# Neighbour lists for a graph network: the second half of each list is traced one list later

## The chip, the cores and the metric

The kernel runs on one core of one Trainium2 chip. The metric is the device time of one execution in microseconds; less is better. Times of the kernel before: 2126.52 us, median of 3 runs (2125.99 to 2130.2).

## The reference

Two layers of graph attention over 4096 nodes, each with a residual and a layer norm. The adjacency matrix is given dense (4096 x 4096 integers), but it is sparse and its density falls with the row and the column number. Cut to what matters here:

```python
e = leaky_relu(f2[:, :, None] + f1[:, None, :], 0.2)     # per head, 4096 x 4096
e = where(adj[None] > 0, e, NEG_INF)
att = softmax(e, axis=-1)
out = einsum('knm,kmp->knp', att, h)                     # h = x @ W, per head
x = layernorm(x + out)                                   # layer 0; layer 1 has two
                                                         # such attentions and two dense layers
```

`adj` is random with probability proportional to 1 / sqrt((i + 1)(j + 1)), so the first 128 rows have up to some hundred neighbours each, the last 128 rows up to two dozen.

## The kernel before

The kernel does not compute the dense 4096 x 4096 scores. A first stage, `find_edges`, turns every block of 128 rows of `adj` into a list of its edges; the three attention layers after it gather the neighbours' rows by these lists. A last stage does the two dense layers. (A dense path exists for inputs that don't fit the lists; a flag chooses it at run time, and it is not taken here.)

`find_edges` handles 35 lists, counted v = 0 to 34 here: the first block of 128 rows is cut into four column ranges (lists 0 to 3), and every block after it is one list (lists 4 to 34, row blocks 1 to 31). k is the most neighbours of a row in a list (104 or 112 in lists 0 to 3, then 56 down to 24), and n the number of chunks of 128 edges that the list takes (12 or 13, then 21 down to 5).

The way of one list, with the lines of the code and the engine that does each step:

- First half. The 2 MB of a row block come in as integers, and ScalarE makes signs of them (`sg`, L848). TensorE makes keys (L877 adds the signs, L878 the column's place) in PSUM, 1024 columns at a time, in two buffers, with four matmuls of 512 columns each. VectorE takes the eight largest keys of every segment of columns (`cand`, L884; in lists 0 to 3 three times, with replacements, L887), and then the k largest of these in order (`lst`, L899 and L901). ScalarE makes of them the column numbers (`qs`, L906) and, by signs with a running sum (L909), the number of neighbours; GpSimd makes the counts of it in six or seven small steps (L911 to L926).
- Second half. TensorE adds up the counts of the rows ahead of each row (`prs`, L931, the prefix sum). ScalarE makes the start and end of each row's edges and, of both, `sides` (L932 to L943); GpSimd adds the two sides to `s1` (L944). ScalarE and GpSimd split `qs` into two bf16 parts (L952 to L955). TensorE multiplies both by `s1` (`pl`, L960 to L969), which gives each edge its row's data, in pieces of at most 512 columns; `pl` has one PSUM buffer. ScalarE copies the node number (`nl`, L971) and for the long lists `kk` (L984). VectorE picks each edge's neighbour (`sel`, L977 to L981, or L986 for lists 0 to 3), and GpSimd writes `hole` and `idx` (L972, L992 to L994), which the gathers use.

Beside the last list of each row block, `beside(t)` loads that block of x, transposes it and multiplies it by the first layer's weights (L683 to L717).

The order of the instructions within this stage isn't written by hand. The tile framework's scheduler sets it when the kernel is built: it walks through the program by estimated durations and gives each engine, whenever that engine is free, the ready instruction that was traced first. What comes out is one fixed queue for each engine. The stages after `find_edges` are traced with `manual_schedule`, so their order is that of the code. There the first gathers are those of row block 31, which is the last list to be made.

Of the kernel before, what the change touches and what calls it, by code (L numbers as in the profile page):

```python
# [10 lines left out]
F32 = mybir.dt.float32  # L11
BF16 = mybir.dt.bfloat16
# [3 lines left out]
AF = mybir.ActivationFunctionType  # L16
OP = mybir.AluOpType
AX = mybir.AxisListType
# [3 lines left out]
P = 128  # L22
N = 4096
# [20 lines left out]
FAR = -1e30  # L44
# [514 lines left out]
def sparse_path(  # L559
# [23 lines left out]
    nc = tc.nc  # L583
# [6 lines left out]
    most = max(p.blocks for p in pts)  # L590
    longest = max(p.n for p in pts)
    kmax = max(p.k for p in pts)
# [8 lines left out]
    ident_b = const.tile([P, P], BF16, name="s_identb")  # L601
# [10 lines left out]
    half = const.tile([P, 2], F32, name="half")  # L612
# [10 lines left out]
    s1 = const.tile([P, blocks_ * P], BF16, name="s1")  # L623
# [227 lines left out]
    def find_edges(big, sb, ps, pk, constants, sg, beside):  # L851
# [8 lines left out]
        starts = big.tile([P, nv], F32, name="starts")  # L860
        ends = big.tile([P, nv], F32, name="ends")
        degsum = big.tile([P, 1], F32, name="degsum")

        for v, p in enumerate(pts):
            t, k, c0, nch = p.t, p.k, p.first, p.n
            if t > 0:
# [28 lines left out]
            last = cand.rearrange("p (s e) -> p s e", e=r8)[:, skip:, r8 - 1]  # L895
# [9 lines left out]
            qs = sb.tile([P, kmax + 1], F32, name="qs")[:, : k + 1]  # L905
# [4 lines left out]
            deg = degs[:, v : v + 1]  # L910
# [16 lines left out]
            else:  # L927
                nc.gpsimd.tensor_copy(counts[:, v : v + 1], deg)
            deg = counts[:, v : v + 1]
            prs = ps.tile([P, 1], F32, name="prs", tag="small")  # L930
            nc.tensor.matmul(prs, before, deg, start=True, stop=True)  # L931
            nc.scalar.activation(qs[:, k:], prs, AF.Identity, bias=ends_at[:, v : v + 1], scale=-1.0)  # L932

            lim = sb.tile([P, 1], F32, name="lim")
            nc.gpsimd.tensor_sub(lim, deg, mids[:, v : v + 1])
            first = starts[:, v : v + 1]
            nc.scalar.activation(first, prs, AF.Identity, bias=mids[:, v : v + 1], scale=-1.0)
            nc.scalar.activation(ends[:, v : v + 1], prs, AF.Identity, bias=lim)
            wide = p.blocks * P
            here = s1[:, p.at * P : p.at * P + wide]  # L940
            sides = sb.tile([P, 2, most * P], BF16, name="sides")[:, :, :wide]
            nc.scalar.activation(sides[:, 0], iota_e[:, :wide], AF.Sign, bias=first)
            nc.scalar.activation(sides[:, 1], iota_e[:, :wide], AF.Sign, bias=ends[:, v : v + 1], scale=-1.0)  # L943
            nc.gpsimd.tensor_add(here, sides[:, 0], sides[:, 1])  # L944


            rhs = sb.tile([P, 2 * (kmax + 2)], BF16, name="rhs")[:, : 2 * (k + 2)].rearrange("p (h w) -> p h w", h=2)
            rest = sb.tile([P, 2 * (kmax + 1)], BF16, name="rest")[:, : 2 * (k + 1)].rearrange("p (h w) -> p h w", h=2)
            q2 = sb.tile([P, 2 * (kmax + 1)], F32, name="q2")[:, : 2 * (k + 1)].rearrange("p (h w) -> p h w", h=2)
            shape = [P, 2, k + 1]  # L950
            for h in range(2):
                nc.scalar.activation(rhs[:, h, : k + 1], qs, AF.Copy, scale=half[:, h : h + 1])  # L952
            nc.gpsimd.tensor_mul(q2, qs[:, None, :].to_broadcast(shape), half[:, :, None].to_broadcast(shape))
            nc.gpsimd.tensor_sub(rest, q2, rhs[:, :, : k + 1])
            nc.gpsimd.tensor_copy(rhs[:, :, k + 1], row1)  # L955
            per = 512 // (k + 2)
            for lo in range(0, nch, per):
                m = min(per, nch - lo)
                pl = ps.tile([P, m, k + 2], F32, name="pl")
                nc.tensor.matmul(  # L960
                    pl, ident_b, own_b[:, None, kmax - k :].to_broadcast([P, m, k + 2]), start=True, stop=False
                )
                last = None
                for block, groups, chunks in blocks_in(p, lo, m):
                    for of, w in ((rhs, k + 2), (rest, k + 1)):
                        if last:
                            nc.tensor.matmul(*last, start=False, stop=False)
                        last = pl[:, chunks, :w], s1[:, ts(p.at + block, P)], of[:, groups, :w]
                nc.tensor.matmul(*last, start=False, stop=True)  # L969
                cs = slice(c0 + lo, c0 + lo + m)  # L970
                nc.scalar.copy(nl[:, cs], pl[:, :, k + 1])  # L971
                nc.gpsimd.tensor_scalar(hole[:, cs, 0], nl[:, cs], -0.5, FAR, op0=OP.is_lt, op1=OP.mult)  # L972
                src = sb.tile([P, longest], F32, name="src")[:, :m]
                sel = sb.tile([P, 512], F32, name="sel")[:, : m * k].rearrange("p (m k) -> p m k", k=k)
                if k < 100:
                    shape = [P, m, k]
                    nc.vector.tensor_tensor(  # L977
                        sel, iota_k[:, lo : lo + m, :k], pl[:, :, k : k + 1].to_broadcast(shape), op=OP.is_equal
                    )
                    nc.vector.tensor_tensor(sel, sel, pl[:, :, :k], op=OP.mult)  # L980
                    nc.vector.tensor_reduce(src, sel, AX.X, OP.add)  # L981
                else:
                    kk = sb.tile([P, longest], F32, name="kk")[:, :m]
                    nc.scalar.copy(kk, pl[:, :, k])  # L984
                    for c in range(m):
                        nc.vector.scalar_tensor_tensor(  # L986
                            sel[:, c], iota_k[:, lo + c, :k], kk[:, c : c + 1], pl[:, c, :k],
                            op0=OP.is_equal, op1=OP.mult, accum_out=src[:, c : c + 1],
                        )

                past = sb.tile([P, longest], F32, name="past")[:, :m]
                nc.gpsimd.tensor_scalar(past, nl[:, cs], -0.5, 2.0 * N, op0=OP.is_lt, op1=OP.mult)  # L992
# [377 lines left out]
    with ExitStack() as pools:  # L1370
        big = pools.enter_context(tc.tile_pool(name="eb", bufs=1))
        sb = pools.enter_context(tc.tile_pool(name="es", bufs=2))
# [3 lines left out]
        ps = pools.enter_context(tc.tile_pool(name="ep", bufs=1, space=PSUM))  # L1376
# [21 lines left out]
    sb = ctx.enter_context(tc.tile_pool(name="ls", bufs=2, reuse_waits="tile"))  # L1398
# [30 lines left out]
    with tc.tile_pool(name="tb", bufs=1, side="right", reuse_waits="tile") as big, \  # L1429
# [95 lines left out]
        for last, block in zip(blocks, blocks[1:]):  # L1525
            chunks = sum(u.n for u in units if u.t in block)
# [91 lines left out]
```

## Time and profile before

| | |
|---|---|
| median of the runs | 2126.52 us |
| the profiled execution, its own time | 2338.45 us |
| its span | 2336.3 us |
| granted TensorE clock, mean | 0.879 |
| busy: PE / DVE / ACT / POOL | 76% / 57% / 28% / 49% |
| `find_edges`, by the trace | from the start to about 505 us |
| busy in its first 505 us: PE / DVE / ACT / POOL | 354.70 / 372.16 / 297.44 / 216.18 us |

PE is TensorE (PEld its weight loads), DVE VectorE, ACT ScalarE, POOL GpSimd, SP the engine that issues most DMAs. In an answer of the trace a name such as `cand<-key` says what is written and what is read. A wait is given as "engine tile line <- the engine, tile and line that ended it". In a timeline each row has the start, the duration, the engine, the line, the operation, the tiles with their shapes, and in square brackets how long the engine was idle before it and what ended that. The profiled execution is about a tenth longer than the median of the runs.

### The profile page before, as it was taken

To read this page: it belongs to the slowest core of one execution; us is meant where nothing else is said; L and a number is where in the kernel's file an instruction comes from. 1 tells how busy PE (TensorE), PEld (TensorE's weight loads), DVE (VectorE), ACT (ScalarE), POOL (GpSimd) and SP (SyncE) were. 2 spreads that over 40 slices of the span, in tenths; PEclk is the share of its full clock that TensorE was granted. 3 is DMA by queue.
4 is the path that set the end of the run, shared out by engine and by line. 5 is a ranking of instruction groups with operands and counts; after the bars stand their busy time and mean duration, and the time that the engine had idled before them with its cause. 6 is when DMAs were issued, how large, how long until landed. Compare 5 with 4: busy or idle time off the path is not lost.

```text
span 2336.3 us, 29301 instructions
## 1 busy us (share of the span) xinstructions
PE 1771.7 (76%) x8987; PEld 1040.1 (45%) x8987; DVE 1331.3 (57%) x3933; ACT 660.7 (28%) x2316; POOL 1151.6 (49%) x1658
## 2 busy tenths in 40 slices
PE   4777776645677787764667687666999898998997
PEld 3655442213444564432444465434545443444444
DVE  5887777745676797744555676653343424334322
ACT  3446776650222222111222232211111011111221
POOL 5424444456555666536556666536355634445300
PEclk9889997866878899876788899887999998999999
DMA  6434565536666667526555556436254624335301
GB/s 214 132 129 158 219 241 220 213 83 179 181 175 182 197 208 224 166 76 163 154 140 145 159 158 186 133 110 191 85 156 126 172 82 148 101 109 150 90 19 51
DMA packets 132589, 351.94 MB, mean 151 GB/s; under 512 B 41922, under 2 KB 42954, under 8 KB 128454
## 3 DMA queue, kind: packets, MB, share of 16 engines
q0 software_dynamic: 74160, 206.25, 32.5%
q1 hardware_dynamic: 58262, 143.72, 17.3%
q8 instruction: 74, 1.21, 0.2%
q14 instruction: 93, 0.76, 0.1%
HBM read 347.31 MB, written 42.24 MB: 167 GB/s over the span
## 4 chain that ended last, share of the span: by engine, by line
PE 46%; DVE 16%; issue 13%; ACT 7%; another core or an unknown queue 7%; POOL 6%; DMA 4%; SPq 0%; DVEq 0%; POOLq 0%; ACTq 0%
PE acc L1220 15%; PE ph L697 11%; PE p L1495 10%; PE p L1507 5%; DVE g L1208 3%; POOL g L1084 2%; DMA xr<-sx_d 2%; DVE cand L884 2%; DMA g<-table_t,idx 2%; PE pt L683 1%; POOL s L944 1%; DVE cand L901 1%; DVE lst L899 1%; ACT sides L943 1%
## 5 line engine op out<-in xcount | busy, mean ns | idle before, releaser
L1084 POOL DMA_INDIRECT g<-table_t,idx x927 | 937.2, 1011 | 769.4 <-PE acc L1220 336.4
L1220 PE MATMUL acc<-g,sm 128*64 128x260 f32 (+2 forms) x4068 | 587.9, 414 | 175.3 <-DVE g L1208 91.7
L697 PE MATMUL ph<-sw_t,xt 128*128 128x264 f32 (+1 forms) x1536 | 436.4, 437 | 146.5 <-ACT xt L686 80.6
L1220 PEld LDWEIGHTS acc<-g,sm 128*64 128x64 f32 x4068 | 332.9, 146 | 395.1 <-issue 123.9
L697 PEld LDWEIGHTS ph<-sw_t,xt 128*128 128x128 f32 x1536 | 323.0, 217 | 229.2 <-ACT xt L686 97.9
L1208 DVE TENSOR_TENSOR g<-g,wp 128x2048 f32<-128x2048 f32 (+4 forms) x134 | 349.3, 2607 | 37.9 <-ACT wp L1163 18.7
L884 DVE MAX8 cand<-key 128x8 f32<-128x353 f32 (+55 forms) x467 | 196.3, 446 | 79.5 <-PE key L878 78.9
L1495 PE MATMUL p<-sht,sl1w 128*128 128x512 f32 (+1 forms) x576 | 229.0, 553 | 5.5 <-issue 4.9
L1507 PE MATMUL p<-sl2w,shid 128*128 128x512 f32 x512 | 227.2, 598 | 0.0
L686 ACT ACTIVATE xt<-pt 128x128 f32<-128x128 f32 x384 | 101.5, 279 | 292.9 <-PE pt L683 122.1
L710 ACT COPY hrow<-ph 128x260 f32<-128x260 f32 (+2 forms) x194 | 71.9, 374 | 320.2 <-PE ph L697 186.9
L1495 PEld LDWEIGHTS p<-sht,sl1w 128*128 128x128 f32 x576 | 107.7, 191 | 116.9 <-issue 112.0
L1507 PEld LDWEIGHTS p<-sl2w,shid 128*128 128x128 f32 x512 | 95.4, 190 | 120.4 <-issue 119.6
L1257 DVE SCALAR_TENSOR_TENSOR o<-ex,o 128x512 f32<-128x512 f32 x64 | 44.5, 695 | 179.2 <-ACT ex L1256 150.0
L877 PE MATMUL key<-sg,s_identb 128*128 128x512 bf16 (+1 forms) x258 | 111.9, 435 | 14.5 <-DVE cand L884 9.0
L848 ACT ACTIVATE sg<-raw 128x4096 bf16<-128x4096 int32 (+1 forms) x39 | 117.0, 2999 | 9.4 <-PE key L877 5.0
L1498 ACT ACTIVATE shid<-p,sl1b 128x512 f32<-128x512 f32 (+1 forms) x72 | 46.0, 640 | 244.5 <-PE p L1495 221.0
L878 PE MATMUL key<-frac,places 128*128 128x512 bf16 (+1 forms) x258 | 112.0, 435 | 2.6 <-POOL places L784 2.6
L1195 DVE TENSOR_SCALAR sm<-iota_n,nl,w 128x64 f32<-128x64 f32 x339 | 83.5, 328 | 31.9 <-ACT w L1166 31.9
L1155 DVE TENSOR_TENSOR z<-s,g 128x16 f32<-128x16 f32 (+9 forms) x294 | 44.7, 174 | 82.9 <-DMA g<-table_t,idx 81.2
L686 ACT ACTIVATION_READ_ACCUMULATOR xt<-pt 128x1 f32 x384 | 79.9, 208 | 0.0
L1228 DVE RECIPROCAL rd<-acc 128x8 f32<-128x8 f32 x64 | 13.1, 205 | 114.4 <-PE acc L1220 73.3
(184 smaller groups left out, 1812.8 us busy)
## 6 DMA issues: line engine op xcount, KB each, us to landing
raw<-in_adj_dram SPq DMA_DIRECT2D x31, 2048.0 KB
table_t<-hrow SPq DMA_DIRECT2D x64, 260.0 KB
xr<-in_x_dram SPq DMA_DIRECT2D x64, 256.0 KB
g<-table_t,idx POOLq DMA_INDIRECT x927
table_t<-hrow SPq DMA_DIRECT2D x32, 257.0 KB
sx_d<-o SPq DMA_DIRECT2D x32, 256.0 KB
xr<-sx_d SPq DMA_DIRECT2D x32, 256.0 KB
out_dram<-xr SPq DMA_DIRECT2D x32, 256.0 KB
```

The lines of the kernel that those rows point to most:

```text
L686: nc.scalar.activation(xt[:, c, :], pt[:, c, :], AF.Copy, accum_out=st.xparts[:, c, t : t + 1])
L697: nc.tensor.matmul(ph[:n], columns(c), st.w[:, c, j], start=(c == 0), stop=(c == FC - 1))
L848: nc.scalar.activation(sg[:, ts(i, w)], raw[:, ts(i, w)], AF.Sign)
L877: nc.tensor.matmul(out_, ident_b, sg[:, j:e], start=True, stop=False)
L878: nc.tensor.matmul(out_, places[:, w], frac[:, j - w * KW : e - w * KW], start=False, stop=True)
L884: nc.vector.max(out=cand[:, at : at + 8], in_=part)
L1084: nc.gpsimd.indirect_dma_start(out=u.g[:, k, : self.st.row], out_offset=None, in_=self.st.table[:, :], in_offset=bass.IndirectOffsetOnAxis ...
L1195: nc.vector.tensor_scalar(sm[:, at + i], of_g, node[k], u.w[:, k], op0=OP.is_equal, op1=OP.mult)
L1208: nc.vector.tensor_mul(body, body, wp[:, :, :, None].to_broadcast(body.shape))
L1220: nc.tensor.matmul(out_[g * HN : (g + 1) * HN], sm[:, slot], rows(k), start=start, stop=stop)
L1495: nc.tensor.matmul(p1, l1w[:, c, ts(k, P)], hts[b][:, c, :n], start=(c == 0), stop=(c == FC - 1))
L1507: nc.tensor.matmul(p2, hids[b][:, k, ts(j, P)], l2w[:, k, :], start=(k == 0), stop=(k == HC - 1))
```

## The change

The second half of each list is put into a function `place`, with all that it uses of its list bound as defaults. The function is kept in a list and called one list later: after the first half of list v + 1, and before `beside` of that list's block. The last one is called after the loop. No instruction is added, removed or altered, and no buffer; only the order in which they are traced. Cut to its core (the body of `place` is L930 to L994 as they were, moved right):

```diff
         degsum = big.tile([P, 1], F32, name="degsum")
 
+        places_of = []
         for v, p in enumerate(pts):
...
             deg = counts[:, v : v + 1]
-            prs = ps.tile([P, 1], F32, name="prs", tag="small")
-            nc.tensor.matmul(prs, before, deg, start=True, stop=True)
...
-                nc.gpsimd.tensor_add(past, past, src)
-                nc.gpsimd.tensor_copy(idx[:, cs], past)
+            def place(v=v, p=p, k=k, c0=c0, nch=nch, qs=qs, deg=deg):
+                prs = ps.tile([P, 1], F32, name="prs", tag="small")
+                nc.tensor.matmul(prs, before, deg, start=True, stop=True)
...
+                    nc.gpsimd.tensor_add(past, past, src)
+                    nc.gpsimd.tensor_copy(idx[:, cs], past)
+
+
+            places_of.append(place)
+            if len(places_of) > 1:
+                places_of.pop(0)()
             if p.last:
                 beside(t)
+        places_of.pop(0)()
```

More of the change, by code (lines that the diff above doesn't have):

```diff
@@ L929, in find_edges @@
             deg = counts[:, v : v + 1]
-            prs = ps.tile([P, 1], F32, name="prs", tag="small")
[L931 to L944, printed above, removed]
@@ L947, in find_edges @@
[L947 to L978, printed above, removed]
-                    )
[L980 to L988, printed above, removed]
-                        )
-                past = sb.tile([P, longest], F32, name="past")[:, :m]
-                nc.gpsimd.tensor_scalar(past, nl[:, cs], -0.5, 2.0 * N, op0=OP.is_lt, op1=OP.mult)
-                nc.gpsimd.tensor_add(past, past, src)
-                nc.gpsimd.tensor_copy(idx[:, cs], past)
@@ new lines, in place @@
+            def place(v=v, p=p, k=k, c0=c0, nch=nch, qs=qs, deg=deg):
+                prs = ps.tile([P, 1], F32, name="prs", tag="small")
+                nc.tensor.matmul(prs, before, deg, start=True, stop=True)
+                nc.scalar.activation(qs[:, k:], prs, AF.Identity, bias=ends_at[:, v : v + 1], scale=-1.0)
+                lim = sb.tile([P, 1], F32, name="lim")
+                nc.gpsimd.tensor_sub(lim, deg, mids[:, v : v + 1])
+                first = starts[:, v : v + 1]
+                nc.scalar.activation(first, prs, AF.Identity, bias=mids[:, v : v + 1], scale=-1.0)
+                nc.scalar.activation(ends[:, v : v + 1], prs, AF.Identity, bias=lim)
+                wide = p.blocks * P
+                here = s1[:, p.at * P : p.at * P + wide]
+                sides = sb.tile([P, 2, most * P], BF16, name="sides")[:, :, :wide]
+                nc.scalar.activation(sides[:, 0], iota_e[:, :wide], AF.Sign, bias=first)
+                nc.scalar.activation(sides[:, 1], iota_e[:, :wide], AF.Sign, bias=ends[:, v : v + 1], scale=-1.0)
+                nc.gpsimd.tensor_add(here, sides[:, 0], sides[:, 1])
+                rhs = sb.tile([P, 2 * (kmax + 2)], BF16, name="rhs")[:, : 2 * (k + 2)].rearrange("p (h w) -> p h w", h=2)
+                rest = sb.tile([P, 2 * (kmax + 1)], BF16, name="rest")[:, : 2 * (k + 1)].rearrange("p (h w) -> p h w", h=2)
+                q2 = sb.tile([P, 2 * (kmax + 1)], F32, name="q2")[:, : 2 * (k + 1)].rearrange("p (h w) -> p h w", h=2)
+                shape = [P, 2, k + 1]
+                for h in range(2):
+                    nc.scalar.activation(rhs[:, h, : k + 1], qs, AF.Copy, scale=half[:, h : h + 1])
+                nc.gpsimd.tensor_mul(q2, qs[:, None, :].to_broadcast(shape), half[:, :, None].to_broadcast(shape))
+                nc.gpsimd.tensor_sub(rest, q2, rhs[:, :, : k + 1])
+                nc.gpsimd.tensor_copy(rhs[:, :, k + 1], row1)
+                per = 512 // (k + 2)
+                for lo in range(0, nch, per):
+                    m = min(per, nch - lo)
+                    pl = ps.tile([P, m, k + 2], F32, name="pl")
+                    nc.tensor.matmul(
+                        pl, ident_b, own_b[:, None, kmax - k :].to_broadcast([P, m, k + 2]), start=True, stop=False
+                    )
+                    last = None
+                    for block, groups, chunks in blocks_in(p, lo, m):
+                        for of, w in ((rhs, k + 2), (rest, k + 1)):
+                            if last:
+                                nc.tensor.matmul(*last, start=False, stop=False)
+                            last = pl[:, chunks, :w], s1[:, ts(p.at + block, P)], of[:, groups, :w]
+                    nc.tensor.matmul(*last, start=False, stop=True)
+                    cs = slice(c0 + lo, c0 + lo + m)
+                    nc.scalar.copy(nl[:, cs], pl[:, :, k + 1])
+                    nc.gpsimd.tensor_scalar(hole[:, cs, 0], nl[:, cs], -0.5, FAR, op0=OP.is_lt, op1=OP.mult)
+                    src = sb.tile([P, longest], F32, name="src")[:, :m]
+                    sel = sb.tile([P, 512], F32, name="sel")[:, : m * k].rearrange("p (m k) -> p m k", k=k)
+                    if k < 100:
+                        shape = [P, m, k]
+                        nc.vector.tensor_tensor(
+                            sel, iota_k[:, lo : lo + m, :k], pl[:, :, k : k + 1].to_broadcast(shape), op=OP.is_equal
+                        )
+                        nc.vector.tensor_tensor(sel, sel, pl[:, :, :k], op=OP.mult)
+                        nc.vector.tensor_reduce(src, sel, AX.X, OP.add)
+                    else:
+                        kk = sb.tile([P, longest], F32, name="kk")[:, :m]
+                        nc.scalar.copy(kk, pl[:, :, k])
+                        for c in range(m):
+                            nc.vector.scalar_tensor_tensor(
+                                sel[:, c], iota_k[:, lo + c, :k], kk[:, c : c + 1], pl[:, c, :k],
+                                op0=OP.is_equal, op1=OP.mult, accum_out=src[:, c : c + 1],
+                            )
+                    past = sb.tile([P, longest], F32, name="past")[:, :m]
+                    nc.gpsimd.tensor_scalar(past, nl[:, cs], -0.5, 2.0 * N, op0=OP.is_lt, op1=OP.mult)
+                    nc.gpsimd.tensor_add(past, past, src)
+                    nc.gpsimd.tensor_copy(idx[:, cs], past)
```

## The prediction

> **What bounds the kernel now.** The change touches one stage only, the making of the neighbour lists, so I first looked for the stage's place in the span. The table of busy time by stretch (columns: stretch, its length, then busy time and count on PE, PEld, DVE, ACT and POOL, granted clock, DMA share, GB/s) gives it:
>
> ```profile
> 35.00:170.00 135.00, 101.69 (x478) 75.69 (x479) 114.61 (x532) 62.27 (x279) 45.15 (x96) 0.87 0.44 143
> 170.00:240.00 70.00, 56.09 (x344) 35.60 (x342) 51.73 (x196) 44.02 (x132) 32.64 (x108) 0.91 0.45 162
> 240.00:505.00 265.00, 185.43 (x896) 86.09 (x895) 189.42 (x612) 180.63 (x416) 112.84 (x423) 0.85 0.52 192
> ```
>
> The stage ends near 505 of 2336.3 us. The gathers of the next layer start with row block 31, whose list is finished last, so a microsecond saved before the last list is saved from the total. DVE is the fullest engine: 114.61 of 135.00 us (85%) in the four lists of row block 0, 189.42 of 265.00 (71%) from about the ninth list on. No engine and no DMA queue is full there, so I went to what the idle time waits for. The answer on waits, DVE alone and then PE alone, from 35 to 505 us (columns: total us, times, longest):
>
> ```profile
> DVE cand L884 <- PE key L878: 73.2, 59, 3.3
> DVE sel L986 <- ACT kk L984: 17.3, 10, 3.5
> DVE sel L977 <- ACT nl L971: 6.0, 6, 2.1
> ```
>
> ```profile
> PE pl L967 <- POOL s L944: 35.7, 32, 4.8
> PE prs L931 <- POOL counts L926: 33.8, 29, 2.1
> PE pl L960 <- DVE sel L980: 7.0, 7, 1.9
> ```
>
> DVE waits 73.2 us for keys that PE makes, while PE waits 35.7 + 33.8 us for steps of the second half (prs, pl). The keys are late because they stand behind a waiting prs or pl in PE's queue. The timeline shows it for row block 30, whose prs cuts one key pair of row block 31 in two:
>
> ```profile
> 484.59 0.63 PE L877 MATMUL key<-sg,s_identb 128*128 128x512 bf16 x1
> ...
> 485.70 0.59 PE L931 MATMUL prs<-counts,before 128*128 128x1 f32 x2 [0.48 <-POOL counts L926]
> ...
> 486.15 0.59 PE L878 MATMUL key<-frac,places 128*128 128x512 bf16 x1
> ...
> 486.78 1.30 DVE L884 MAX8 cand<-key 128x8 f32<-128x949 f32 x2 [1.85 <-PE key L878]
> ```
>
> The key matmuls around it follow one another at 0.43 us; the second of this pair starts 1.56 us after the first, and DVE loses 1.85 us. In row block 0 the same happens on DVE itself, where a sel step waits with maxima of the next list behind it:
>
> ```profile
> 48.50 0.23 DVE L887 MATCH_REPLACE8 left<-cand,left 128x85 f32<-128x85 f32 x1
> 50.97 0.32 DVE L986 SCALAR_TENSOR_TENSOR sel<-iota_k,kk,pl 128x104 f32<-128x104 f32 x1 [2.24 <-ACT kk L984]
> ...
> 51.95 0.25 DVE L884 MAX8 cand<-left 128x8 f32<-128x85 f32 x1
> ```
>
> **What the Trainium skill says.** "PSUM — Partial Sum Buffer", section "Engine vs sequencer instructions": the queues of ScalarE, VectorE and GpSimdE are strict FIFO, and matmuls start and complete in program order. The trace agrees: L878 at 486.15 follows the prs at 485.70 although its input was there. So what the scheduler writes down is what the chip waits in. "Perfetto Trace Analysis", section "Optimization Strategy": gaps that repeat can mean too few buffers for the next tile. pl has one buffer, and PE waits 7.0 us for it. "TensorE: Matmul & The Clock Gate", section "What's actually happening": the clock gate lets through half of the clock after an idle window. The trace has both speeds, key matmuls that start 0.43 us apart (484.17, 484.59) and 0.21 apart (477.77, 477.99), and a granted clock of 0.85 from 240 us on. No page prices a reordering.
>
> **The change, part by part.** It removes and adds no instruction. place(v), from prs to idx, is traced after the first half of list v+1 and before the projection beside it. Trace order is what the scheduler ranks by when two instructions are ready together, so place(v) now ranks below keys, maxima, sorted list and counts of list v+1 (and below the projection of its own block), and still above keys of list v+2. An engine without ready work of higher rank takes place(v) as before. place issues no DMA: no load or store on SP's queue and no gather on POOL's is passed. What is passed, engine by engine:
>
> *DVE, row block 0 (lists 0 to 3).* The ten waits of L986 are 17.3 us. Four are the first piece of a list (2.24, 1.44, 1.94 and 3.48, sum 9.1): the scheduler put them as soon as it held them ready, the chip was later. With lower rank they come only into gaps between a maximum and its replacement, so some max work goes ahead. The later pieces wait for one another through the single pl buffer, whatever their rank. I take half of 9.1: **-4.5 us**; bounds 0 (the gaps come at once) and -17.3 (every wait covered).
>
> *PE, lists 4 to 33.* I counted in the PE timeline how many of the 16 key matmuls of list v+1 precede prs of list v. A group that shares one key buffer is four matmuls, and in 18 of 30 lists the count is 8 or 12: the next group waits for a buffer and the rank decides nothing. In 12 lists it is 9, 10, 11, 13 or 14: there prs has cut into a ready group. After the change the one to three remaining matmuls (0.21 to 0.43 us each) go first and fill the wait for counts, 1.17 us on average (33.8 / 29), so prs isn't later, and DVE gets its keys up to 1.2 us earlier (73.2 / 59 is the mean wait): at most 12 x 1.2 = 14.4. But there is a second chain: pl(v) stands in front of keys(v+2), whose first maximum DVE takes before the sorted list of v+1, which leads to counts, prs and pl of v+1. Place(v) keeps its rank over keys(v+2), so this chain stays. I take half: **-7 us**; bounds 0 and -14.4.
>
> *DVE, lists 4 to 34.* sel(v) now ranks below the sorted list of v+1 (L899, L901). At its start two or three of the three L899 have already gone in most lists with k = 24, so it moves little there. The single pl buffer comes free later, and L960 of the next list waits at PE with keys behind it: today 7.0 us. If it moves by one L899/L901 pair, 0.5 us, in all 31 lists, it costs 15.5; the nearer value is a fifth: **+3 us**; bounds -1 and +15.5 (a wait for nl, 6.0 us in all, may also shrink).
>
> *ACT and POOL.* Seven short ACT steps and nine POOL steps of place rank below qs, signs and six small POOL steps of list v+1 (about 0.8 and 1.3 us). POOL is busy 112.84 of 265 us and the two groups lie several us apart, so I cost it at 0, hidden by POOL's idle time; if they met in every list, 31 x 1.3 = 40 us of delay would lie on place, which has nearly a list's time of slack. The 3.6 us sign step of list v+2 is in front of or behind place(v) exactly as before.
>
> *The end.* The sorted list of block 31 no longer shares DVE with sel of block 30 (three steps of 0.28, 0.26 and 0.27 us, today inside it): -0.5; bounds -1 and +2, if place(30) spills behind it. The last place itself has nothing to hide behind either way.
>
> Sum: -4.5 - 7 + 3 - 0.5 = **-9 us**. The durations come from the profiled execution, 2338.45 us by its own time for a span of 2336.3, and 10% above the median of 2126.52; I subtract the same microseconds from the median, since the page doesn't show which stage is longer under the profiler (scaled by 0.91 it would be -8): 2126.5 - 9 = about **2118 us**.
>
> **The rivals.**
> 1. *The order hardly moves* (21%). For it: 18 of 30 counts are 8 or 12, sel already comes after most of the sorted list, and engines with idle time take ready work whatever its rank. Against it: 12 cut groups and 17.3 us of waits for kk. Time 2126, within 4 us.
> 2. *The pl buffer becomes the wait* (33%), the case on the slower side. The place is L960 and L967 at the head of PE's queue. With sel(v) behind the sorted list of v+1, and in lists 4 to 6 (two or three pl pieces each, 0.4 to 0.65 us per sel step) behind up to a list's maxima, the bank comes free later than PE reaches it; keys of v+2 stand behind it, and DVE starves. One more wait of 0.5 us in 31 lists is 15.5 us; less the 2 us gained at row block 0 it is about 2140. It decides from the point where L980 of list v ends later than the last key group of v+1 on PE.
> 3. *The circle is cut* (9%). If the lists shift so that the first key group of v+2 goes ahead of pl(v), the chain above is broken for good and the list runs at DVE's busy time: half of 73.2 + 17.3 is 45 us, 2081. Against it: place(v) keeps its rank over keys(v+2).
>
> **How the numbers follow.** My own case has 37%. About 0.2%, 4.3 us, is what a measurement of this kernel can tell from no change. Faster by more: 31 of my 37, all 9 of rival 3, 3 of rival 1: 43%. Within: 6 + 14 + 2 of rival 2: 22%. Slower: 31 of rival 2 and 4 of rival 1: 35%. Range: my case alone reaches from 2103 (all gains near their ends) to 2124; rival 2 with an ACT or POOL collision in a few lists reaches 2143, and part of rival 3 goes down to 2092; that leaves about 2 in 10 outside.
>
> **What the profile after would show.** Right: waits of L986 for kk under 13 us; prs of a list only after 4, 8, 12 or 16 key matmuls of the next; waits of L884 for L878 down by about 7 us from 73.2; the stage over 8 to 10 us earlier. Wrong: waits of L960 for sel well above 7.0 us (rival 2), or a stage end within 4 us with the same counts (rival 1), or pl(v) behind keys of v+2 (rival 3). A difference that arises after the stage would make the whole account wrong.

## The result, and the profile after

The kernel after the change takes 2121.22 us (median of 8 runs, 2116.87 to 2122.94), the kernel before, beside it, 2127.68 us (8 runs, 2125.99 to 2133.16). The ratio is 0.9964, 95% interval 0.9953 to 0.9975. By the medians 6.5 us are saved, 0.3%; by the ratio it would be 7.7 us. The profiled execution of after took 2116.87 us (span 2114.9), the lowest of its runs.

The profile of before had a span of 2336.3 us. Some chips ran slower: the kernel before takes 2128 us beside the runs e1 to e4 below (one chip), but 2319 to 2320 us beside e5 to e12 (two others), and the profile of before is of the slower kind. Nearly all of that difference lies behind the list stage (1833 us from the first gather on, against 1624 us in the profile of after). So profiles are compared in the list stage alone, and runs by their ratio to runs of the kernel before on the same chip.

First the last row of the table of busy time by stretch, after the change (columns as in the prediction: stretch, length, busy time and count on PE, PEld, DVE, ACT and POOL, granted clock, DMA share, GB/s):

```profile
240.00:505.00 265.00, 180.73 (x893) 85.47 (x891) 187.26 (x612) 189.19 (x414) 119.27 (x431) 0.85 0.55 199
```

The totals hardly tell the two kernels apart: DVE is busy 187.26 of the last 265 us, 189.42 before. A fixed stretch cuts a shifted kernel at another place in its work. A better clock is the start of the layer's first gather, which needs the last list. It is the first number of the range in the answer on the tile g, before and then after:

```profile
L1084 POOL DMA_INDIRECT g<-table_t,idx x927: 996/1002/1503, 502.9 to 2205.7; - x186
```

```profile
L1092 POOL DMA_INDIRECT g<-table_t,idx x927: 992/998/1597, 491.2 to 1982.6; - x186
```

502.9 became 491.2: the stage ends 11.7 us earlier. That is 5 us more than the medians show, and the profiled execution of after was itself 4.4 us under its median. In a second pair of profiles (e9, e10) the same difference is 7.6 us.

The answer on waits of after, DVE alone and then PE alone, 35 to 505 us (total us, times, longest):

```profile
DVE cand L885 <- PE key L879: 70.1, 56, 3.8
DVE sel L988 <- ACT kk L986: 18.1, 9, 4.1
DVE sel L979 <- ACT nl L973: 5.5, 6, 1.6
```

```profile
PE pl L969 <- POOL s L946: 34.3, 30, 2.4
PE prs L933 <- POOL counts L927: 30.7, 29, 2.1
PE pl L962 <- DVE sel L982: 2.2, 2, 1.6
```

Only one wait has clearly gone: pl for its buffer (L962, L960 before), 7.0 to 2.2 us. The wait for kk, which the prediction wanted under 13 us, is 18.1. The wait for keys fell by 3.1 us, not by 7. To see why the time fell all the same, the stage has to be cut by the progress of its lists. I took the start of each list's prs from the trace, the first list being 0:

| | prs(2) at | prs(2) to prs(9) | prs(9) to prs(34) | prs(34) to first gather |
|---|---|---|---|---|
| before | 124.3 | 124.6 | 245.3 | 8.7 |
| after | 117.1 | 131.4 | 234.9 | 7.8 |
| difference | -7.2 | +6.8 | -10.4 | -0.9 |
| second pair of profiles (e10 less e9) | -4.3 | +5.8 | -8.2 | -0.9 |

Three things happen. Row block 0 gains 4 to 7 us, lists 3 to 9 lose nearly all of it, and the 25 lists from 9 to 34 gain 8 to 10 us. In that last stretch alone (249 to 494 us before, 249 to 483 us after) the waits for keys are, before and then after:

```profile
DVE cand L884 <- PE key L878: 62.7, 51, 3.3
```

```profile
DVE cand L885 <- PE key L879: 52.3, 47, 2.8
```

10.4 us less, just what the stretch is shorter. (DVE's own busy time in it is the same, 177.4 us before and 176.6 after.) Between 172 and 249 us the same wait rose from 10.4 to 16.5 us, which is why the sum over the stage hides it.

The timeline of PE after the change, at a prs near the end of the stage:

```profile
463.84 0.61 PE L878 MATMUL key<-sg,s_identb 128*128 128x512 bf16 x1 [0.36 <-DVE cand L885]
464.24 0.63 PE L879 MATMUL key<-frac,places 128*128 128x512 bf16 x1
464.66 0.63 PE L878 MATMUL key<-sg,s_identb 128*128 128x512 bf16 x1
465.09 0.59 PE L879 MATMUL key<-frac,places 128*128 128x512 bf16 x1
...
466.52 0.38 PE L933 MATMUL prs<-counts,before 128*128 128x1 f32 x2 [0.79 <-POOL counts L927]
466.77 0.38 PE L878 MATMUL key<-sg,s_identb 128*128 128x512 bf16 x1
```

The group of four key matmuls is whole, and the 0.79 us that prs waits fall between two groups. In the order in which PE takes its instructions, prs of the lists 4 to 33 now stands behind 8, 12 or 16 key matmuls of the next list, in every one; before it was 9, 10, 11, 13 or 14 in 12 of them.

### The profile page after: what moved, and what is told of

The parts are those of the page before. It is cut to its first block, busy times and chain, and to the rows that moved or that the text cites. A ratio compares the mean times of both kernels' runs of the same rounds, so it can differ in the third digit from the quotient of the medians.

```text
span 2114.9 us, 29298 instructions
## 1 busy us (share of the span) xinstructions
PE 1710.6 (81%) x8987; PEld 1000.7 (47%) x8987; DVE 1321.9 (63%) x3933; ACT 663.0 (31%) x2316; POOL 1151.0 (54%) x1658
## 4 chain that ended last, share of the span: by engine, by line
PE 35%; DVE 18%; issue 15%; POOL 13%; DMA 11%; ACT 6%; SPq 0%; POOLq 0%; DVEq 0%; ACTq 0%
PE acc L1228 10%; PE p L1503 10%; DMA g<-table_t,idx 9%; POOL g L1092 8%; PE ph L697 6%; DVE g L1216 5%; PE p L1515 4%; DVE cand L885 2%; POOL s L946 1%; DMA xr<-sx_d 1%; ACT sides L945 1%; DVE sm L1195 1%; PE key L879 1%; POOL sprod L667 1%; DVE cand L902 1%
## 5 line engine op out<-in xcount | busy, mean ns | idle before, releaser
L1228 PE MATMUL acc<-g,sm 128*64 128x260 f32 (+2 forms) x4068 | 573.7, 412 | 179.3 <-DVE g L1216 143.4
L1228 PEld LDWEIGHTS acc<-g,sm 128*64 128x64 f32 x4068 | 325.0, 146 | 394.9 <-DVE g L1216 163.5
L697 PE MATMUL ph<-sw_t,xt 128*128 128x264 f32 (+1 forms) x1536 | 399.5, 408 | 52.7 <-ACT xt L686 45.8
L697 PEld LDWEIGHTS ph<-sw_t,xt 128*128 128x128 f32 x1536 | 295.6, 199 | 122.6 <-ACT xt L686 66.8
L1163 DVE TENSOR_TENSOR z<-s,g 128x16 f32<-128x16 f32 (+9 forms) x294 | 47.2, 174 | 154.7 <-DMA g<-table_t,idx 147.9
L848 ACT ACTIVATE sg<-raw 128x4096 bf16<-128x4096 int32 (+1 forms) x39 | 116.9, 2997 | 10.4 <-PE key L878 6.7
L1171 ACT ACTIVATE wp<-z 128x32 f32<-128x32 f32 (+4 forms) x134 | 27.5, 205 | 233.8 <-DVE g L1216 233.8
L1520 DVE TENSOR_TENSOR xr<-p,xr 128x512 f32<-128x512 f32 x32 | 22.0, 688 | 95.1 <-PE p L1515 94.3
```

Source lines behind the costliest of these rows:

```text
L697: nc.tensor.matmul(ph[:n], columns(c), st.w[:, c, j], start=(c == 0), stop=(c == FC - 1))
L848: nc.scalar.activation(sg[:, ts(i, w)], raw[:, ts(i, w)], AF.Sign)
L1228: nc.tensor.matmul(out_[g * HN : (g + 1) * HN], sm[:, slot], rows(k), start=start, stop=stop)
```

## The experiments

My theory after the result: a prs that waits for its counts in the middle of a ready group holds up keys that DVE needs, and the change puts prs between groups. Rivals: it is the later pl and sel that matter (e3); it is row block 0 (e1 against e2); only the place of prs in time matters, not whether it cuts a group (e5, e6). Behind them stands a larger question, that of the prediction's third rival: do prs and pl, which PE waits for some 65 us, hold the whole stage in a circle (e4, e7, e8, e11, e12)?

All results in one table. "Stretch" is prs(9) to prs(34); the three waits are those in that stretch, in us: DVE for keys, PE's prs for counts, PE's pl for s. "Saved" is measured against the kernel before on the same chip: the difference of the medians for after and e1 to e4 (2128 us before), the ratio applied to 2319 or 2320 us for e5 to e12, whose runs scatter more. Times in the expectations are on the scale of 2128 us.

| run | ratio to before, 95% interval | saved, us | first gather at | prs(2) to prs(9) | stretch | keys | counts | s |
|---|---|---|---|---|---|---|---|---|
| before | | | 502.9 | 124.6 | 245.3 | 62.7 | 28.5 | 22.6 |
| after | 0.9964, 0.9953 to 0.9975 | 6.5 | 491.2 | 131.4 | 234.9 | 52.3 | 22.7 | 26.3 |
| e1_front | 0.9975, 0.9964 to 0.9986 | 5.2 | 495.6 | 126.8 | 243.2 | 62.2 | 32.2 | 20.0 |
| e2_rest | 0.9966, 0.9955 to 0.9978 | 7.8 | 493.6 | 125.2 | 237.5 | 55.0 | 22.4 | 24.4 |
| e3_pl_only | 1.0006, 0.9996 to 1.0016 | -1 | 500.7 | 128.4 | 245.8 | 58.2 | 31.9 | 24.7 |
| e4_lag2 | 0.9892, 0.9875 to 0.991 | 22.8 | 480.2 | 119.5 | 230.8 | 55.9 | 47.2 | 0 |
| e5_whole12 | 0.9965, 0.9942 to 0.9988 | 8 | 488.0 | 126.5 | 235.4 | 51.1 | 20.1 | 26.2 |
| e6_cut10 | 0.997, 0.9949 to 0.9992 | 7 | 489.9 | 123.6 | 241.1 | 59.8 | 24.7 | 24.9 |
| e7_whole16 | 0.9996, 0.9976 to 1.0016 | 1 | 503.6 | 132.4 | 242.0 | 24.4 | 2.6 | 17.1 |
| e8_lag2_whole16 | 0.9977, 0.9957 to 0.9996 | 5 | 498.0 | 123.1 | 243.8 | 61.8 | 0 | 43.1 |
| e9_before_again | 1.0004, 0.9984 to 1.0024 | -1 | 501.1 | 125.6 | 243.8 | 61.3 | 27.2 | 24.9 |
| e10_after_again | 0.9968, 0.9948 to 0.9989 | 7 | 493.5 | 131.4 | 235.6 | 52.8 | 22.7 | 26.6 |
| e11_lag2_whole12 | 0.9871, 0.9831 to 0.9911 | 30 | 469.9 | 117.2 | 223.2 | 47.6 | 18.2 | 0 |
| e12_lag3 | 0.9928, 0.9903 to 0.9952 | 17 | 482.1 | 120.1 | 232.0 | 55.2 | 51.9 | 0 |

A 0 stands for a wait that the answer does not list. The stretch of one program moves by 1.5 us (before, e9) and 0.7 us (after, e10) from profile to profile, the first gather by 1.8 and 2.3 us. That is the measure for all differences below; every other kernel has one profile.

### The two halves of the change: e1 and e2

e1 delays place for lists 0 to 3 only, e2 from list 4 on.

```diff
-            if len(places_of) > 1:
-                places_of.pop(0)()
+            while len(places_of) > (1 if v < 4 else 0):      # e1; in e2: (0 if v < 4 else 1)
+                places_of.pop(0)()
```

> Only the second halves of lists 0 to 3 (row block 0) are traced one list later; from list 4 on each second half is traced at once, as before. Theory A (the gain is made on PE, where prs no longer cuts a group of keys in lists 4 to 33): 0 to -2 us against before, and the counts of keys ahead of prs are again odd ones in about a dozen lists. Theory B (the gain is made in row block 0, on DVE): -5 to -7 us, the whole of it. Theory C (any new order moves the time by a few us, either way): anything from -8 to +8 us.

> Lists 0 to 3 as before, and only from list 4 on is the second half traced one list later. Theory A: -5 to -9 us against before, at least as much as the whole change, and every prs comes after 4, 8, 12 or 16 keys of the next list. Theory B: 0 to -1 us. Theory C: not to be told beforehand, -8 to +8 us.

Each half alone saves about what the whole does: 5.2 and 7.8 us, sum 13.0, against 6.5. So e1 came as theory B said and e2 as theory A said, and neither theory holds alone. The trace says where each gets it. e1 has the early prs(2) (117.5 us) and a stretch hardly shorter than before's (243.2). e2 has a late prs(2) (122.5) and the short stretch (237.5). The whole has both, and then loses the first one between lists 2 and 9, where it takes 131.4 us against 126.8 and 125.2 in the halves. Row block 0's gain is real, but the full change doesn't keep it.

### Which part of place: e3

prs, the sides and the bf16 parts are given to the scheduler at once, as before; only pl, sel and idx come one list later.

```diff
             def place(...):
                 ...
                 nc.gpsimd.tensor_copy(rhs[:, :, k + 1], row1)
+                return lambda: late(v, p, k, c0, nch, rhs, rest)
+
+            def late(v, p, k, c0, nch, rhs, rest):
                 per = 512 // (k + 2)
...
-            places_of.append(place)
+            places_of.append(place())
```

> The second half is cut once more: prs to the two bf16 parts are traced at once, as before, and only the pl matmuls, sel and idx one list later. If the rank of prs against the keys is what counts (theory A), this gives 0 to -2 us against before and prs cuts groups of keys again. If it is the rank of sel on DVE (sorted list first, the step that I had put down as a cost), it gives the whole gain, -5 to -8 us, and the waits of the pl matmul for sel fall from 7.0 us to about 2 us as they did in the change.

Nothing is saved (1.0006). From 35 to 485 us the waits are

```profile
DVE cand L885 <- PE key L879: 71.7, 58, 3.5
...
PE prs L933 <- POOL counts L927: 38.4, 30, 2.8
```

and in PE's order prs cuts groups again (9, 10, 11 or 13 key matmuls ahead of it in 11 lists). prs(2) is early all the same (118.4 us, after 117.1, before 124.3): row block 0's gain belongs to the later pl and sel, and the gain from list 9 on doesn't come without a later prs (or later ACT and POOL steps up to the bf16 parts, which e3 leaves early together with prs).

### Whole groups against cut groups: e5 and e6

Both are the kernel after the change with the place of prs(v) set by hand, by an order edge behind the fifth 512-wide piece of the next list's keys. In e5 prs is then offered last, behind all keys, and stands behind 12 of 16 key matmuls in all but two lists. In e6 it is offered inside the key loop and stands behind 10, 11 or 13 in 21 of 30 lists.

```diff
 # e5
-                nc.tensor.matmul(prs, before, deg, start=True, stop=True)
+                with tc.issue_after(keys_of[v + 1][:5][-1][1].ins):
+                    nc.tensor.matmul(prs, before, deg, start=True, stop=True)
 # e6, in the loop over the key pieces
+                    if v and len(key_ops) == 5:
+                        sum_up(v - 1, key_ops[-1][1])   # prs of list v - 1, same edge
```

> The kernel after the change, with one more order edge: the prefix sum's matmul prs(v) may not be issued on PE before the fifth 512-wide piece of list v+1's keys. In PE's program every prs(v) of lists 4 to 33 (but two) then stands behind exactly 12 of the 16 key matmuls of list v+1, so always between two whole groups of four; in the kernel after the change 8 and 12 are mixed. Theory (a prs that waits for its counts costs only where it stops key matmuls that could have been issued): as the kernel after the change or a little better, 2112 to 2122 us, PE waiting 25 to 31 us for counts. Rival (only how late prs comes counts, since what follows it is the critical way): prs is later in 9 lists, so 2120 to 2128 us.

> The kernel after the change, but prs(v) alone is given to the scheduler inside list v+1's keys, right after the fifth 512-wide piece, with the same order edge; all that follows it keeps its place one list later. In PE's program prs(v) then stands behind 10, 11 or 13 of the 16 key matmuls of list v+1 in 21 of the lists 4 to 33, so it cuts a group of four whose other keys could be issued; in 9 lists it stands behind 12. Against e5_whole12 the only difference is this. Theory (a cut group costs DVE about 0.6 us a list): 21 cut lists cost some 12 us over e5_whole12: about 2127 to 2134 us, DVE waiting over 73 us for keys. Rival (an earlier prs helps the chain prs, s, pl, which PE waits for with 34 us): 2110 to 2120 us, below e5_whole12. Second rival (the rank of prs against the keys never mattered, the time came from pl and sel): equal to e5_whole12 within 3 us.

The answer on waits from 35 to 485 us, of e5 and then of e6:

```profile
DVE cand L887 <- PE key L880: 61.1, 53, 3.3
```

```profile
DVE cand L896 <- PE key L887: 68.4, 60, 3.9
```

And one cut in the timeline of e6:

```profile
464.60 0.39 PE L886 MATMUL key<-sg,s_identb 128*128 128x512 bf16 x1 [0.71 <-DVE cand L896]
466.11 0.59 PE L869 MATMUL prs<-counts,before 128*128 128x1 f32 x2 [1.12 <-POOL counts L940]
466.56 0.59 PE L887 MATMUL key<-frac,places 128*128 128x512 bf16 x1
```

The second half of the pair (L887) had nothing to wait for and starts 1.96 us after the first. That costs: in the stretch DVE waits 59.8 us for keys instead of 51.1, in 16 cut lists, and the stretch is 5.7 us longer, nearly four times its scatter. Counted list by list (the waits in front of the maxima of lists 10 to 34), all of it lies in those 16 lists, where 30.5 us became 39.3; in the nine others it is 21.7 and 21.5. So a cut group does cost, about 0.5 us of DVE's waiting and on average 0.35 us of time per cut list. The time isn't lost evenly, though: from prs(9) to prs(21), with nine cut lists, e6 loses nothing against e5 (it is 0.4 us ahead), and all of the loss comes after that. And my expectation, a time above before's and over 73 us of waits for keys, was wrong. e6 came 3.7 us sooner to list 9 than e5, the first gathers lie only 1.9 us apart, and the runs do not tell the two apart. Why e6 is quicker in lists 2 to 9 I did not find. e5's own time lies where the theory's band and its rival's overlap and decides nothing; its stretch answers a side question: prs later in ten lists (12 keys ahead of it in place of 8) cost nothing.

### prs behind all keys: e7

The same edge, on the last key.

```diff
-                with tc.issue_after(keys_of[v + 1][:5][-1][1].ins):
+                with tc.issue_after(keys_of[v + 1][-1][1].ins):
```

> The kernel after the change, with the order edge on the last key of list v+1: prs(v) stands behind all 16 key matmuls of list v+1 in every list. PE no longer waits for counts (30.7 us before the edge, expected under 8), and no keys are held up by prs. Theory of the circle (place(v)'s pl comes later, and the keys of list v+2 are held behind it): what PE saves in front of prs it waits in front of pl for s, 34 us rising to 45 to 60, and the time is 2118 to 2135 us. Rival (the wait for counts in front of keys is all that matters): 2095 to 2108 us.

PE's wait for counts is gone, and so is most of DVE's wait for keys, yet nothing is saved (0.9996). From 35 to 485 us:

```profile
DVE sel L985 <- ACT nl L979: 54.6, 31, 3.5
...
DVE cand L887 <- PE key L880: 27.3, 39, 2.1
PE pl L975 <- POOL s L952: 26.7, 21, 2.8
```

DVE now waits 54.6 us for nl, a step that follows pl. PE's wait for s did not rise to 45 to 60 us as the theory had it (26.7); another 29.8 us PE waits for `rest`, the second bf16 part. Time moved from one wait in the way of prs and pl to another: what prs loses, pl and sel lose too. Of the places of prs that were tried with one list of lag, those between whole groups at 8 to 12 keys are the best. One more thing stands in this trace: pl(v) comes behind 8 to 14 of the 16 keys of list v + 2 in nearly every list, so the condition of the prediction's third rival is met, and nothing is saved.

### Two and three lists of lag: e4, e8, e11, e12

e4 delays place by two lists and gives qs a third buffer. Then pl(v) comes behind half of the keys of list v + 2 (8 matmuls nearly everywhere). e12 delays by three.

```diff
-            qs = sb.tile([P, kmax + 1], F32, name="qs")[:, : k + 1]
+            qs = sb.tile([P, kmax + 1], F32, name="qs", bufs=3)[:, : k + 1]     # e12: bufs=4
...
-            if len(places_of) > 1:
+            while len(places_of) > 2:                                           # e12: > 3
```

> The second half is traced two lists later (the buffers of qs are three in place of two, as it lives longer). Now the keys of list v+2 rank above pl of list v as well. If the chain pl(v), keys(v+2), first maximum, sorted list of v+1, counts, prs, pl(v+1) holds the lists at their period, cutting it gives much more: -20 to -45 us against before, and DVE's waits for keys fall from about 70 us to under 45 us. If engines with idle time take place(v) as soon as it is ready whatever its rank, the order hardly differs from a lag of one: -4 to -9 us.

> The kernel with a lag of three lists (qs in four buffers): prs(v) again behind 8 or 12 key matmuls of list v+1, pl(v) behind all 16 of list v+2. Theory (a lag of two already took pl out of the circle, so what is left is the wait of prs for counts, which a longer lag does not touch because prs is still put ahead of keys(v+1)): PE waits 45 to 65 us for counts, under 5 us for s, and the time is within 5 us of the lag of two, 0.987 to 0.992 of before. Rival (each list of lag takes further waits away): 8 to 20 us faster than the lag of two, 0.980 to 0.985 of before. A loss is possible at the end, where three places follow the last list instead of two.

e4 saves 22.8 us, some three times the change. The time came into the first band, but the waits for keys, expected under 45 us, did not. The waits of e4 from 35 to 485 us:

```profile
DVE cand L885 <- PE key L879: 66.4, 45, 4.4
...
PE prs L933 <- POOL counts L927: 54.6, 27, 4.4
...
PE pl L969 <- POOL s L946: 3.6, 3, 2.8
```

pl waits 3.6 us for s instead of 34: it is out of the circle. What is left is prs, and it waits longer than ever. The timeline of PE in e4 shows both:

```profile
440.23 0.19 PE L969 MATMUL pl<-rhs,s 128*128 128x52 bf16 x1
440.25 0.18 PE L971 MATMUL pl<-rest,s 128*128 128x50 bf16 x1
442.89 0.59 PE L933 MATMUL prs<-counts,before 128*128 128x1 f32 x2 [2.45 <-POOL counts L927]
443.34 0.59 PE L878 MATMUL key<-sg,s_identb 128*128 128x512 bf16 x1
```

pl follows the keys without a gap, then prs stands 2.45 us at the head of the queue with keys behind it. From list 9 to 34 PE's two waits together are hardly less than after the change (47.2 us, 49.0 after), and DVE waits no less for keys (55.9, 52.3 after). Most of what e4 gains over after lies earlier: from prs(2) to prs(9) it takes 119.5 us instead of 131.4, with less waiting for keys (10.5 us, 17.7 after) and for kk (7.9, 11.5 after). From list 9 to 34 it gains 4.1 us, and at the end, with two places left, it loses 3.4 (prs(34) to the first gather, 11.2 us instead of 7.8).

A third list of lag adds nothing: e12's first gather is at 482.1 us (e4 480.2), its wait for counts 51.9 us in the stretch (47.2). Its ratio, 0.9928, lies just outside the theory's band on the slow side, far from the rival's.

So I combined the two findings: two lists of lag, and prs held back to the last key (e8) or to 12 keys of 16 (e11), with the edges of e7 and e5.

> The kernel with a lag of two lists (e4_lag2) and the same order edge: prs(v) behind all 16 key matmuls of list v+1, pl(v) behind 12 to 16 key matmuls of list v+2. Theory: in e4_lag2 the wait of PE for counts (54.6 us up to 485 us) is what is left of the circle, and the edge takes it away: PE waits for counts under 10 us, DVE for keys 45 to 55 us instead of 66, and the time is 2085 to 2098 us. Rival (DVE's own work is the bound once pl is out of the way, the wait for counts is idle time that nobody needs): 2101 to 2108 us, as e4_lag2.

> The kernel with a lag of two lists and the order edge on the fifth 512-wide piece of list v+1's keys: prs(v) behind exactly 12 of 16 key matmuls of list v+1 in every list, pl(v) behind 8 of list v+2. With no edge prs stands behind 8 or 12 and PE waits 54.6 us for counts; with the edge at 16 that wait went to pl, 52.4 us for s. Theory of the circle over two lists: the middle place shortens both, PE waiting 15 to 35 us for counts and under 10 us for s, DVE for keys 45 to 58 us, and the time is 6 to 20 us under the lag of two without the edge: 2085 to 2099 us, or 0.980 to 0.987 of before. Rival (prs pays its wait wherever it stands, since counts come late): within 4 us of the lag of two without the edge, 0.9875 to 0.991 of before.

e8 missed both of its bands. It saves 5 us only, since PE's wait has gone over to pl once more:

```profile
DVE cand L887 <- PE key L880: 76.6, 47, 4.9
PE pl L975 <- POOL s L952: 52.4, 29, 4.0
```

s itself is late there: from prs to the end of s it takes 7.5 us on average over lists 9 to 33, against 3.5 in e4. e11 hits the middle. From 35 to 485 us:

```profile
DVE cand L887 <- PE key L880: 54.3, 43, 4.1
...
PE prs L937 <- POOL counts L929: 19.0, 17, 2.0
...
PE pl L975 <- POOL s L952: 2.9, 3, 2.1
```

Both waits of PE are short at once. The stretch takes 223.2 us, 22 less than before and 7.6 less than e4, and the first gather starts at 469.9 us, 33 us earlier than before. The interval of its ratio (0.9831 to 0.9911) spans both bands that were expected, so against e4 it is the trace, not the runs, that tells them apart. Against both kernels of this case it is faster, clear of the noise: 0.9871, some 30 us.

### How steady the profiles are: e9 and e10

Before and after once more, unchanged.

> The kernel before the change once more, for a second profile of its list stage: how far two profiles of one program differ. The first showed prs(9) to prs(34) in 245.3 us and the first gather 513.8 us after the trace's first record. If the stage is steady, the second gives 245.3 within 2 us and 513.8 within 4 us, and the gains of the other kernels in that stretch (10.5 us for the change, 9.9 us with prs behind 12 keys, 4.2 us with cut groups) are told apart by one profile each; if it differs by over 4 us in the stretch, the 5.7 us between the last two say nothing. Time: 0.998 to 1.002 of before.

> The kernel after the change once more. If the profiles are steady: prs(9) to prs(34) in 233 to 237 us, DVE waiting for keys in that stretch 50 to 54 us (52.3 in its first profile, 62.7 before), and the time 5 to 9 us under before. If the lead of row block 0 (7 us at list 2, 0 at list 9 in its first profile) was lost by chance, prs(9) comes at 252 to 256 us this time; if the change's order loses it, again at 258 to 261 us.

Stretches of 243.8 and 235.6 us, waits for keys of 61.3 and 52.8: both as expected, and the ratio of e10 (0.9968) agrees with the first result. On the clock of the expectation, which begins about 11 us ahead of the page's, prs(9) came at 261.3 us, just past the second band and far from the first. So the loss of row block 0's lead belongs to the order that the change makes and not to chance.

## Why the prediction was right, and where not

The forecast of 2118 us, 9 us less, met 2121. Its sum holds, but of its larger terms only the one on PE was in the main what I said it was.

- **DVE, row block 0, -4.5 us: right at list 2, lost by list 9. The steps moved as forecast, but the waits that priced the term did not fall.** prs(2) came 7.2 us earlier (4.3 in the second pair). The sel steps did go into the gaps between a maximum and its replacement: up to prs(2), 18 of 25 of them came directly behind another sel in the kernel before (and in e2), none of 25 after (nor in e1 and e3). But the first step of a piece can stand where it stood, and it waits as long, as the timeline of DVE after shows:

```profile
47.99 0.23 DVE L888 MATCH_REPLACE8 left<-cand,left 128x85 f32<-128x85 f32 x1
50.45 0.32 DVE L988 SCALAR_TENSOR_TENSOR sel<-iota_k,kk,pl 128x104 f32<-128x104 f32 x1 [2.23 <-ACT kk L986]
...
50.70 0.24 DVE L885 MAX8 cand<-left 128x8 f32<-128x85 f32 x1
...
51.41 0.30 DVE L988 SCALAR_TENSOR_TENSOR sel<-iota_k,kk,pl 128x104 f32<-128x104 f32 x1
```

  The wait is 2.24 us before and 2.23 after; only the next maximum now starts behind the first sel step and not behind four of them. In all, the waits for kk rose from 17.3 to 18.1 us. The step of the prediction that failed is the price, half of the four first-piece waits: that it came near 4 us is luck. Of the lead at prs(2), 3.6 us are less idle time of DVE (12.6 us from 42 to 117 us, against 16.2 from 42 to 124) and 3.6 less busy time for nearly the same instructions; in the second pair 0.9 and 3.4. From list 2 to list 9 the lead was lost: DVE waits 17.7 us for keys there instead of 10.4, and 11.5 for kk instead of 8.5. e1 and e5 keep 4 to 5 us of it at list 9, so it can be kept; which step of the order loses it in after is open.
- **PE, lists 4 to 33, -7 us: right in kind, and in size for the cut lists; a part of the gain has no term.** The counts of 9, 10, 11, 13 and 14 are gone. The wait for keys from list 9 to 34 fell by 10.4 us (8.5 in the second pair), more than the half that I took. Inside the stretch from a list's first to its last maximum, DVE's idle time went from 1.64 to 1.06 us per list (1.47 to 1.08 in the second pair, lists 9 to 33). But counted list by list, as for e6, the 12 lists that prs had cut have 6.5 us of a fall of 8.8 (5.2 of 8.0 in the second pair). That is 0.4 to 0.5 us per cut list, near the 0.6 that I took and near what e6 shows. The other 2.3 us (2.8) fell in the 13 lists that were not cut. The time can't be laid to the cut lists either: from prs(9) to prs(13), where before cuts no group, after gains 3.8 us (2.9), and from prs(28) to prs(34), where before cuts six in a row, 0.7 (0.7). So cut groups are shown to cost DVE waits, and they explain the larger part of the fall, but not all of it. In e6, with more cut groups than before, the stretch is still 3 to 4 us shorter than before's. What makes up this rest no run separates; place also ranks below the projection of its own block, and its ACT and POOL steps come later.
- **The pl buffer, +3 us, and the second rival (33%, about 2140 us): did not come.** The wait of L962 for sel fell from 7.0 to 2.2 us. I had reasoned that sel would come later and free the bank later. But pl's first matmul comes later too: it now starts 3.6 us ahead of the end of s instead of 4.7 (means over lists 9 to 33), and hardly ever finds the bank still taken.
- **ACT and POOL, 0: right.** From prs to the end of s it takes 3.65 us instead of 3.49, and from the first small step of the counts to prs 1.50 as before (means over lists 9 to 33).
- **The end, -0.5 us: right.** From prs(34) to the first gather 7.8 us instead of 8.7.
- **Rival 1 (21%, the order hardly moves): fell,** by the counts and by a ratio whose interval lies below 0.998.
- **Rival 3 (9%, the circle is cut): rightly not the case here.** In 27 of 29 lists pl(v) still comes behind at most four keys of list v+2. It pointed to the larger gain, but putting keys(v+2) ahead of pl(v) isn't enough: e7 does it and saves nothing, since sel then holds DVE up. With place two lists later e4 saves 22.8 us, and e11, which eases the wait of prs as well, 30. The 45 us of that rival were too many, because DVE still waits 47.6 us for keys in e11's stretch.

So the -9 of the forecast stand against -7 + 7 - 10 - 1, about -11.7, in the first pair of profiles and -4 + 6 - 8 - 1, about -7.6, in the second: a term that was undone, a stretch that gained more than forecast, and a cost (+3) that never came. The kind of the change was foreseen; that the sum came so near is in part luck.

## What to carry to other kernels

When an engine takes its instructions in a written order, ask of every wait what stands behind it: an instruction that waits about 1 us between two buffer groups cost nothing here that could be seen (after, e5), the same one inside a ready group cost the next engine about 0.5 us each time (e6), and one that waits over 2 us costs between groups too (e4 against e11). Moving the second half a further list away gained more here than ranking it one list lower did (22.8 against 6.5 us), and after each move the wait turned up at another step (counts, s, rest, nl), until prs and pl were both given room. When a fall has been found, count it by the places where the supposed cause is at work and by those where it is not: here a quarter to a third of it lay where no group had been cut. To see what a reordering did, cut the trace by the progress of the work, not by fixed times, since totals over a stage hide a gain and a loss of the same size.

## What the runs showed of the hardware that was not expected

The list stage takes nearly the same time in two runs of one kernel that differ by 9% as a whole. The kernel after the change had its first gather at 491.2 us in a run of 2116.87 us and at 493.5 us in one of 2313.23 us (e10); from there to the end it took 1624 and 1818 us. In the first 490 us the granted clock was 0.88 and 0.87; from 1000 to 1500 us it was 0.94 in the first run and 0.85 in the second, with 2486 and 2140 matmuls recorded. What sets the lower clock there, and whether it is the whole of the difference, these runs do not show.
